# First group's ScalarE opening and small loads, the last group's bias, and one weight tile of layer one in a two-layer graph kernel

## The chip, the cores and the metric

One core of a Trainium2 chip runs the whole kernel in one launch. The metric is device time in microseconds (us). The kernel before takes 3325.39 us, the median of three runs (3324.43 to 3325.61).

## The reference

Two graph layers over 4096 nodes of 512 features, each followed by a residual and a layer norm. All data are float32; `adj` is 4096 x 4096 of zeros and ones.

```python
# layer 0: four heads of 128
support = (x @ weight).reshape(N, 4, 128)                # "s" products in the kernel
f1, f2 = support . weight_u, support . weight_v          # two numbers for each node and head
w = leaky_relu(f1 + f2, slope 0.2) * adj                 # softmax over w where it is not zero
out = softmax(w) @ support + bias + x @ proj_w + proj_b  # "b" products: x @ proj_w
x = layernorm(x + out)
# layer 1: eight heads of 64, keys, queries and values from Wks, Wqs, Wvs
scores = q k^T / 8 + 0.01 * eye - 1e16 * (1 - max(adj, eye))
x = layernorm(x + (softmax(scores) @ v) @ Wo)
```

The residual `x +` of layer 0 is put into `proj_w` as an added identity. `bias` and `proj_b` are both one row of 512 numbers, the same for each node.

## The kernel before

Everything is in `tile_gat_then_masked_attention`; the order of instructions on each engine is that of the Python code, since the schedule is manual. Semaphores between engines follow from the tiles.

**Projections.** Eight groups of 512 nodes (`for g in range(NG)`). Each group makes two results, kind `"s"` (x @ weight, kept as `s4`) and kind `"b"` (x @ (proj_w + identity), kept as `base`). Each is computed by Strassen's scheme in seven smaller products numbered 1 to 7, so a group has 14 calls of `product`, called s1, s5, ... and b1, b5, ... below. A product is eight matmul groups on TensorE (L846). Products 2, 3 and 4 accumulate on the PSUM tiles of 1, 5 and 7, after these have been read: tile 1 by a ScalarE copy (L863), tile 5 also (L863), tile 7 by VectorE (L869), after which GpSimd adds product 5 to the corner (L871). The list that gives the order is `begin` for group 0 (all s, then all b, each 1, 2, 5, 6, 7, 3, 4), `usual` for groups 1 to 6 and `end` for group 7. Products are made of sums of blocks of x (`combine_x`: sums 0 and 1 on VectorE, L797 and L799; 2 and 3 on GpSimd, L801 and L804), and sums of blocks of the weights (`combine_w`, L763), made once. `add_identity` (L895) puts the identity into `pw_sb` by sixteen small GpSimd operations.

`dots` (L817) takes the products of `s4` with `weight_u` and `weight_v` on VectorE. These two rows are loaded into `uv`, copied into PSUM by ScalarE (L928, `uv_ps`) after the seventh product of group 0, and read from there. In group 0 the four calls of `dots` come behind the eighth to eleventh product; the third of them reads the corner that GpSimd made in L871.

`bb` holds bias + proj_b: `bias` is loaded into all partitions (L677), `proj_b` is added to it by an accumulating DMA that GpSimd issues (L905). It is added to `base` by GpSimd (L879), in the last group by VectorE; then SyncE stores `base` to `base_d[g]` in DRAM (L881).

**The first loads.** ScalarE's own queue issues, in this order: four loads of the first half of `weight`, one of x, four of the second half of `weight`, two for `uv`, one for `bb`. ScalarE's first computing instruction is the copy of s1, behind them all.

**Layer 0's attention.** 16 passes (four blocks of 1024 target nodes, four heads), each of 32 steps j over the source nodes. `front(w, h, j)` makes the tile `p` of a step on VectorE (L640), and for even j the mask `az` (L635) out of signs that ScalarE makes (L624); p has four buffers. `front` runs three steps ahead of the matmuls of L1087 (`LA = 3`). For the first pass the fronts of steps 0, 1 and 2 are already called in the last group (`early`); that of step 3 is called in the loop's first turn, behind the last group's work. `beside_unit` puts other work beside the steps: adjacency blocks of the next pass are narrowed (DMA by GpSimd, L586), transposed (DMA by SyncE, L594) and copied to 8 bits by ScalarE (L600), the values of the next head are loaded (L1002). At a block's end `add_base` adds `base_d` to the result by an accumulating DMA (L1063); group 7's is read in the last block only.

**Layer 1** follows: keys, queries and values (L1248 to L1298), then 32 pairs of query group and head pair, in which TensorE makes scores (L1138) and weighted sums (L1599).

Of the kernel before, what the change touches and what calls it, by code (L numbers as in the profile page):

```python
# [8 lines left out]
F32 = mybir.dt.float32  # L9
# [3 lines left out]
AF = mybir.ActivationFunctionType  # L13
ALU = mybir.AluOpType
# [4 lines left out]
P = 128  # L19
# [410 lines left out]
def tile_gat_then_masked_attention(  # L430
# [56 lines left out]
    total = const.tile([P, NG * NP1], F32, name="total")  # L487

    base_d = [dram.tile([P, GT, D], F32, name=f"base_d{g}") for g in range(NG)]
    x1_d = [dram.tile([G, D], F32, name=f"x1_d{g}") for g in range(NG)]  # L490
    sup_d = [dram.tile([P, NT, W0], F32, name=f"sup_d{h}") for h in range(H0)]
    fr_d = [dram.tile([2, H0, W], F32, name=f"fr_d{w}") for w in range(NW)]
# [74 lines left out]
    with tc.tile_pool(name="l0", bufs=NG) as l0, \  # L567
# [77 lines left out]
        with tc.tile_pool(name="l0s", bufs=2) as sp:  # L645
# [14 lines left out]
            def load_w0(queue, dst, src, c):  # L660

                for a in range(NQ):
                    f = a * P + 2 * c * SQ
                    queue.dma_start(
                        dst[a * SQ:(a + 1) * SQ, 2 * c:2 * c + 2, :],
                        src[f:f + 2 * SQ, :].rearrange("(k r) d -> r k d", r=SQ))

            bb = sp.tile([P, D], F32, name="bb", bufs=1)
            load_w0(nc.scalar, w_sb, weight, 0)
            load_x(0, 0, HG // SQ, (nc.sync, nc.sync, nc.sync, nc.scalar))  # L670
            load_w0(nc.scalar, w_sb, weight, 1)
            load_x(0, HG // SQ, G // SQ)
            for c in range(2):
                load_w0(nc.sync, pw_sb, proj_w, c)
            for k, src in enumerate((weight_u, weight_v)):
                nc.scalar.dma_start(uv[:, k, :], on_all_partitions(src, D))
            nc.scalar.dma_start(bb, on_all_partitions(bias, D))  # L677
            load_x(1)

            def factors(g, s4):  # L680
# [41 lines left out]
            for c in range(NCJ):  # L722
# [4 lines left out]
                if c < NCJ - 3:  # L727
                    for k in range(CJ):
# [1 line left out]
                            lambda c=c, k=k: shrink(0, c, k))  # L730
            beside.setdefault(NT // 2, []).append(lambda: load_fr(0, 0))
            early = {5: lambda: signs(0, 0, 0), 8: lambda: front(0, 0, 0), 9: lambda: front(0, 0, 1),
                     7: lambda: signs(0, 0, 2), 11: lambda: front(0, 0, 2)}

            def turn_x(g, c, n=0, halves=1):

# [98 lines left out]
            def product(g, s4, kind, i):  # L835

                if i in (1, 5, 6, 7):
                    tiles[kind, i] = op.tile([P, G], F32, name="o_ps")  # L840
                out = tiles[kind, {2: 1, 3: 5, 4: 7}.get(i, i)]
                more = i in (2, 3, 4)
                xb, wb = x_of(g, i), w_of(kind, i)
                for t in range(2):
                    for c in range(2):
                        nc.tensor.matmul(out[:, t * HD:(t + 1) * HD], xb[:, c, t * P:(t + 1) * P],  # L846
                                         wb[:, c, :], start=not more and t == 0 and c == 0,
                                         stop=c == 1, skip_group_check=True)
                if i == 1:
                    if kind == "b":  # L850
                        for n in range(2):
                            base[n] = sp.tile([P, 2, D], F32, name="base", bufs=3)
                    elif g == NG - 1:
                        places = room("y_sb").rearrange("p s c r -> p s (c r)")
                        sb.update({("s", 1): places[:, 0], ("s", 5): places[:, 1],
                                   ("b", 1): places[:, 2], ("b", 5): places[:, 3]})
                    else:
                        sb.update({("s", 1): room("z"), ("s", 5): room("z"),
                                   ("b", 1): room("az"), ("b", 5): room("az")})
                u2, p5 = sb[kind, 1], sb[kind, 5]  # L860
                last = block_of(kind, s4, 1, 1)
                if i in (1, 5):
                    nc.scalar.activation(sb[kind, i], out, AF.Copy)  # L863
                elif i == 2:
                    nc.scalar.activation(block_of(kind, s4, 0, 0), as_block(out, kind), AF.Copy)
                elif i == 6:
                    nc.vector.tensor_tensor(u2, out, u2, op=ALU.add)
                elif i == 7:
                    nc.vector.tensor_tensor(last, as_block(out, kind), as_block(u2, kind),  # L869
                                            op=ALU.add)  # L870
                    nc.gpsimd.tensor_tensor(last, last, as_block(p5, kind), op=ALU.add)  # L871
                else:
                    n, m = (0, 1) if i == 3 else (1, 0)
                    nc.vector.tensor_tensor(block_of(kind, s4, n, m), as_block(out, kind),
                                            as_block(u2, kind), op=ALU.add)
                if kind == "b" and i in (3, 4):
                    n = (3, 4).index(i)
                    engine = nc.vector if g == NG - 1 else nc.gpsimd
                    engine.tensor_tensor(base[n], base[n],  # L879
                                            bb[:, None, :].to_broadcast([P, 2, D]), op=ALU.add)  # L880
                    later.at(1, lambda t=base[n]: nc.sync.dma_start(  # L881
                        base_d[g][:, 2 * n:2 * n + 2, :], t))

# [12 lines left out]

            combine_x(0, 0)
            combine_w(nc.vector, "s", (5,))
            for i in (1, 2, 3):
                combine_x(0, i)  # L900
            combine_w(nc.vector, "s", (6, 7, 4))
            for m in range(2):
                add_identity(m)
# [1 line left out]
            nc.gpsimd.dma_start(bb, on_all_partitions(proj_b, D), accum_op=ALU.add)  # L905
            uv_ps = [xp.tile([P, H0, D0], F32, name="x_ps") for _ in range(2)]
            usual = [(kind, i) for i in (1, 5, 2, 6, 7, 3, 4) for kind in ("s", "b")]
            begin = [(kind, i) for kind in ("s", "b") for i in (1, 2, 5, 6, 7, 3, 4)]
            end = [(kind, i) for kind in ("s", "b") for i in (1, 5, 2, 6, 7, 3, 4)]
            for g in range(NG):  # L910
                fs[g] = l0.tile([P, 2, GT, H0], F32, name="f")
                s4 = sp.tile([P, H0, GT, W0], F32, name="s4")
                plan = end if g == NG - 1 else usual if g else begin
                todo = {}
                for k, (i, wait, n, m) in enumerate(
                        ((2, 1, 0, 0), (3, 0, 0, 1), (7, 3, 1, 1), (4, 0, 1, 0))):
                    todo.setdefault(plan.index(("s", i)) + wait if g else 7 + k, []).append((n, m))
                for k, (kind, i) in enumerate(plan):
                    if k in (0, 3, 7, 10):
                        t = (0, 3, 7, 10).index(k)  # L920
                        if t == 1 and g + 2 < NG:
                            load_x(g + 2)
                        for fn in beside.get(g * GT + t, []):
                            fn()
                    product(g, s4, kind, i)
                    if g == 0 and k == 6:
                        for n in range(2):
                            nc.scalar.activation(uv_ps[n], uv[:, n, :].rearrange(  # L928
                                "p (h d) -> p h d", h=H0), AF.Copy)
                    for nm in todo.get(k, ()):  # L930
                        dots(g, s4, *nm)
                    if g == NG - 1 and k in early:
                        early[k]()
                    if g == NG - 1 and k == 10:
                        factors(g, s4)
                    first = 0 if g else 10
                    if g + 1 < NG and first <= k < first + KC:
                        turn_x(g + 1, k - first)
                    if g + 1 < NG and (6 <= k < 10 if g else k == 13):
                        for n in (k - 6,) if g else range(4):  # L940
                            combine_x(g + 1, n)
                    if k in (2, 6, 9, 12):
                        later.step()
                xTs.pop(g)
                x_s.pop(g)
                if g + 1 == NG:
                    later.step()
                if g + 1 < NG:
                    later.at(1, lambda g=g, s4=s4: factors(g, s4))
# [34 lines left out]
        with wait_by_tile("l0v", 2) as vp:  # L984
            pools[1] = vp, vp

            def beside_unit(w, h, j):

                n = w * H0 + h
                if n == 0:  # L990
                    for c, first in zip(range(NCJ - 3, NCJ), (9, 15, 22)):
                        if c > NCJ - 3 and j == first - 7:
                            turn_in0(0, c)
                        if first <= j < first + CJ:
                            shrink(0, c, j - first)
                    if j == LA:
                        narrow(0, NCJ - 1)
# [78 lines left out]
            for n, (w, h, j) in enumerate(steps):  # L1076
                if n + LA < len(steps):
                    beside_unit(*steps[n + LA])
                    front(*steps[n + LA])
                if j == 0:  # L1080
                    o_t[w, h] = [op.tile([P, G], F32, name="o_ps")[:, 0:BK * W0].rearrange(
                        "p (b d) -> p b d", b=BK) for _ in range((WT + BK - 1) // BK)]
# [709 lines left out]
```

## Time and profile before

| what | value |
|---|---|
| median of three runs | 3325.39 us |
| time of the profiled execution | 3324.41 us |
| its span | 3322.5 us |
| TensorE busy | 3301.6 us, 99% of the span |
| VectorE, ScalarE, GpSimd busy | 75%, 59%, 65% |
| mean granted TensorE clock | 0.998 |
| DMA, mean over the span | 184 GB/s |

The page divides the span into 40 slices. TensorE has a 9 (90% or more) in all of them but the last. The time of the profiled execution is 1.91 us more than its span. A share of busy time is a mean over stages, so the questions of this case are read from the list of TensorE's waits and from the order of time in the first 50 us, around 210 us (where layer 0's attention begins) and around 290 us (its second pass).

### The profile page before, as it was taken

To read this page: it belongs to the slowest core of one execution; us is meant where nothing else is said; L and a number is where in the kernel's file an instruction comes from. 1 tells how busy PE (TensorE), PEld (TensorE's weight loads), DVE (VectorE), ACT (ScalarE), POOL (GpSimd) and SP (SyncE) were. 2 spreads that over 40 slices of the span, in tenths; PEclk is the share of its full clock that TensorE was granted. 3 is DMA by queue.
4 is the path that set the end of the run, shared out by engine and by line. 5 is a ranking of instruction groups with operands and counts; after the bars stand their busy time and mean duration, and the time that the engine had idled before them with its cause. 6 is when DMAs were issued, how large, how long until landed. Compare 5 with 4: busy or idle time off the path is not lost.

```text
span 3322.5 us, 67217 instructions
## 1 busy us (share of the span) xinstructions
PE 3301.6 (99%) x27160; PEld 1967.0 (59%) x27160; DVE 2477.7 (75%) x3186; ACT 1947.7 (59%) x2439; POOL 2173.3 (65%) x1602
## 2 busy tenths in 40 slices
PE   9999999999999999999999999999999999999998
PEld 8899999999999777733333333333333333333333
DVE  6689899899999677467767666677666766667766
ACT  1267968878766310156656566566665656656564
POOL 5630040040030244389999999999999999999996
PEclk9999999999999999999999999999999999999999
DMA  8989796686532444489898988889889799897984
GB/s 178 227 204 183 220 182 170 153 191 147 138 93 58 104 146 125 153 221 208 193 211 224 228 195 198 209 188 259 198 197 211 187 215 242 196 210 185 214 195 112
DMA packets 398993, 612.06 MB, mean 184 GB/s; under 512 B 167632, under 2 KB 248528, under 8 KB 398672
## 3 DMA queue, kind: packets, MB, share of 16 engines
q0 software_dynamic: 97520, 258.77, 42.8%
q1 hardware_dynamic: 299280, 345.88, 33.5%
q8 instruction: 216, 3.54, 0.4%
q10 hardware_dynamic: 1872, 3.02, 0.4%
q14 instruction: 105, 0.86, 0.1%
HBM read 315.87 MB, written 109.25 MB: 128 GB/s over the span
## 4 chain that ended last, share of the span: by engine, by line
PE 97%; DVE 1%; DMA 1%; POOL 1%; issue 0%; ACT 0%; ACTq 0%; POOLq 0%; DVEq 0%
PE o_ps L1087 27%; PE o_ps L1599 26%; PE s_ps L1138 26%; PE o_ps L846 5%; PE s_ps L1663 3%; PE s_ps L1298 2%; PE s_ps L1248 2%; PE s_ps L1255 2%; PE x_ps L1255 1%; PE x_ps L1248 1%; PE s_ps L1618 1%; DMA p<-p 0%; PE s_ps L1294 0%; DMA w_sb<-in_L_gnn_weight_dram 0%; DVE p L1731 0%
## 5 line engine op out<-in xcount | busy, mean ns | idle before, releaser
L1574 POOL TENSOR_TENSOR q_sum<-q_sum,p 128x1024 f32<-128x1024 f32 x538 | 1375.6, 2557 | 64.3 <-DMA p<-p 39.5
L1554 DVE TENSOR_TENSOR p<-s_ps,adjT 128x1024 f32<-128x1024 f32 x896 | 1044.5, 1216 | 465.0 <-ACT s_ps L1551 436.2
L1551 ACT ACTIVATE s_ps<-s_ps 128x1024 f32<-128x1024 f32 x1021 | 967.2, 1006 | 594.4 <-PE s_ps L1138 591.9
L1599 PE MATMUL o_ps<-p,v_sb 64*64 64x512 f32 x8192 | 943.6, 590 | 0.0
L1138 PE MATMUL s_ps<-q_sb,k_sb 64*64 64x512 f32 x8192 | 942.9, 589 | 0.1
L1087 PE MATMUL o_ps<-sup_t,p 128*128 128x129 f32 x8192 | 915.7, 275 | 1.2 <-DVE p L640 1.2
L1087 PEld LDWEIGHTS o_ps<-sup_t,p 128*128 128x128 f32 x8192 | 915.3, 192 | 1.7 <-DVE p L640 1.4
L640 DVE SCALAR_TENSOR_TENSOR p<-fr_t,dj,az 128x1024 f32<-128x1024 f32 x512 | 650.3, 1284 | 66.9 <-PE o_ps L1087 38.8
L1599 PEld LDWEIGHTS o_ps<-p,v_sb 64*64 64x64 f32 x8192 | 310.3, 133 | 570.6 <-issue 560.6
L1138 PEld LDWEIGHTS s_ps<-q_sb,k_sb 64*64 64x64 f32 x8192 | 312.6, 133 | 566.4 <-issue 453.9
L624 ACT ACTIVATE z<-fr_t,f 128x1024 fp8e4<-128x1024 f32 x512 | 557.1, 1143 | 100.9 <-DVE az L635 100.8
L1584 POOL DMA_DIRECT2D p<-p x412 | 438.6, 1303 | 10.1 <-PE o_ps L1599 9.2
L1063 POOL DMA_DIRECT2D agg<-base_d x32 | 29.1, 1217 | 386.8 <-DMA sup_t<-sup_d 204.7
L585 POOL COPY seen<-token 128x1 f32<-128x1 f32 x24 | 10.9, 455 | 356.8 <-DVE token L583 356.8
L1554 DVE TENSOR_TENSOR p<-s_ps,md 128x1024 f32<-128x1024 f32 x128 | 150.7, 1217 | 67.8 <-ACT s_ps L1551 62.0
L635 DVE TENSOR_TENSOR az<-adjT,z 128x512 int32<-128x512 int32 x256 | 175.2, 685 | 2.1 <-ACT z L624 0.9
L600 ACT ACTIVATE adjT<-stage 128x1024 fp8e4<-128x1024 bf16 x128 | 130.9, 1051 | 18.3 <-DMA stage<-adj_d 18.2
L1663 PE MATMUL s_ps<-wo_sb,on 128*128 128x512 f32 x240 | 110.8, 604 | 0.0
L1633 ACT ACTIVATE r<-r_h 32x256 f32<-32x256 f32 x248 | 102.2, 412 | 2.9
L1049 ACT ACTIVATE agg<-o_ps,rinv 128x128 f32<-128x128 f32 x128 | 42.1, 370 | 70.5 <-DVE den L1042 46.3
L1322 ACT ACTIVATE v<-s_ps 128x256 f32<-128x256 f32 x28 | 10.7, 383 | 115.0 <-PE s_ps L1298 99.9
L1663 PEld LDWEIGHTS s_ps<-wo_sb,on 128*128 128x128 f32 x240 | 43.3, 189 | 55.9 <-issue 55.7
(275 smaller groups left out, 2236.0 us busy)
## 6 DMA issues: line engine op xcount, KB each, us to landing
p<-p POOLq DMA_DIRECT2D x412, 512.0 KB, 9.1
k_sb<-k_d SPq DMA_DIRECT2D x128, 512.0 KB
v_sb<-v_d SPq DMA_DIRECT2D x128, 512.0 KB
adj_d<-in_adj_dram POOLq DMA_DIRECT2D x32, 1024.0 KB, 11.0
sup_t<-sup_d SPq DMA_DIRECT2D x120, 258.0 KB
fr_t<-fr_d SPq DMA_DIRECT2D x16, 1024.0 KB
adjT_d<-adjT SPq DMA_DIRECT2D x32, 512.0 KB
adjT<-adjT_d SPq DMA_DIRECT2D x32, 512.0 KB
```

The lines of the kernel that those rows point to most:

```text
L624: nc.scalar.activation(z[:, k, :], fr_t[w, h][:, 0, :], AF.Sign, bias=fs[j // GT][:, 0, (j + k) % GT, h:h + 1], saturate=False)
L635: nc.vector.tensor_tensor(az.bitcast(I32), adjT[w, j // CJ][:, j % CJ:j % CJ + 2, :].bitcast(I32), z.bitcast(I32), op=ALU.bitwise_and)
L640: nc.vector.scalar_tensor_tensor(p, fr[:, 1, :], dj[j // GT][:, j % GT, h:h + 1], az_t[w, h, j // 2][:, j % 2, :], op0=ALU.max, op1=ALU.mult)
L846: nc.tensor.matmul(out[:, t * HD:(t + 1) * HD], xb[:, c, t * P:(t + 1) * P], wb[:, c, :], start=not more and t == 0 and c == 0, stop=c == ...
L1087: nc.tensor.matmul(o[t // BK][:, t % BK, :], p[:, t * P:(t + 1) * P], s, start=(j == 0 and t % BK == 0), stop=(j == NT - 1), skip_group_ch ...
L1138: nc.tensor.matmul(s[c:c + MS, e, :], k[r, a + c:a + c + MS], qt[g, m][r, :], start=True, stop=True)
L1551: nc.scalar.activation(s, s, AF.Exp, scale=float(KD) ** -0.5)
L1554: nc.vector.tensor_tensor(p, s, keep[:, None, :].to_broadcast([P, HP, G]), op=ALU.mult)
L1574: nc.gpsimd.tensor_tensor(q, q, p, op=ALU.add)
L1584: later.at(2, lambda: nc.gpsimd.dma_start(a, b, accum_op=ALU.add))
L1599: nc.tensor.matmul(o[c, n, :], v[r, j % CH, c], p[r, e, :], start=(j == 0), stop=(j == NT - 1))
L1663: nc.tensor.matmul(s, on_t[g][:, m, t * P:(t + 1) * P], wo_sb[:, m, :], start=(m == 0), stop=(m == NP1 - 1))
```

## The change

- ScalarE gets a copy of one column, before the loads of the second half of `weight` and behind those of the first.
- The loads of `weight_u`, `weight_v` and `bias` go from ScalarE's queue to GpSimd: the first two between GpSimd's parts of `combine_x` (2 and 3), the third behind part 3.
- Group 0's b products run in the order 1, 5, 2, 6, 7, 3, 4.
- In group 7 `bb` is no longer added to `base`. `bb` is stored to `bb_d` in DRAM in group 1 (SyncE), and in the second pass GpSimd issues a DMA that adds `bb_d`, repeated for the four node tiles, to `base_d[7]` in DRAM.
- The front of step 3 is called in the last group, behind product b3, and no longer in the loop's first turn. (This is the "layer one's fourth weights" of the change's name: the weights of the first attention layer.)

```diff
+    bb_d = dram.tile([P, D], F32, name="bb_d")
...
             load_w0(nc.scalar, w_sb, weight, 0)
             load_x(0, 0, HG // SQ, (nc.sync, nc.sync, nc.sync, nc.scalar))
+            nc.scalar.activation(small.tile([P, 1], F32, name="bn_ve"), ones[:, 0:1], AF.Copy)
             load_w0(nc.scalar, w_sb, weight, 1)
             load_x(0, HG // SQ, G // SQ)
             for c in range(2):
                 load_w0(nc.sync, pw_sb, proj_w, c)
-            for k, src in enumerate((weight_u, weight_v)):
-                nc.scalar.dma_start(uv[:, k, :], on_all_partitions(src, D))
-            nc.scalar.dma_start(bb, on_all_partitions(bias, D))
             load_x(1)
...
             early = {5: lambda: signs(0, 0, 0), 8: lambda: front(0, 0, 0), 9: lambda: front(0, 0, 1),
-                     7: lambda: signs(0, 0, 2), 11: lambda: front(0, 0, 2)}
+                     7: lambda: signs(0, 0, 2), 11: lambda: front(0, 0, 2), 12: lambda: front(0, 0, 3)}
...
                 if kind == "b" and i in (3, 4):
                     n = (3, 4).index(i)
-                    engine = nc.vector if g == NG - 1 else nc.gpsimd
-                    engine.tensor_tensor(base[n], base[n],
-                                            bb[:, None, :].to_broadcast([P, 2, D]), op=ALU.add)
+                    if g < NG - 1:
+                        nc.gpsimd.tensor_tensor(base[n], base[n],
+                                                bb[:, None, :].to_broadcast([P, 2, D]),
+                                                op=ALU.add)
...
             combine_w(nc.vector, "s", (5,))
-            for i in (1, 2, 3):
+            for i in (1, 2):
                 combine_x(0, i)
+            for k, src in enumerate((weight_u, weight_v)):
+                nc.gpsimd.dma_start(uv[:, k, :], on_all_partitions(src, D))
+            combine_x(0, 3)
+            nc.gpsimd.dma_start(bb, on_all_partitions(bias, D))
             combine_w(nc.vector, "s", (6, 7, 4))
...
-            begin = [(kind, i) for kind in ("s", "b") for i in (1, 2, 5, 6, 7, 3, 4)]
             end = [(kind, i) for kind in ("s", "b") for i in (1, 5, 2, 6, 7, 3, 4)]
+            begin = [("s", i) for i in (1, 2, 5, 6, 7, 3, 4)] + end[7:]
...
+                    if (g, k) == (1, 7):
+                        nc.sync.dma_start(bb_d, bb)
                     product(g, s4, kind, i)
...
                 n = w * H0 + h
+                if n == 1 and j == 4 * LA:
+                    nc.gpsimd.dma_start(base_d[NG - 1], bb_d[:, None, :].to_broadcast([P, GT, D]),
+                                        accum_op=ALU.add)
...
                     beside_unit(*steps[n + LA])
-                    front(*steps[n + LA])
+                    if n:
+                        front(*steps[n + LA])
```

## The prediction

> **What bounds the kernel now.** I read the page first, then the list of TensorE's waits, then the timeline of the three places that the change touches. The page says that TensorE is the bound throughout: busy 99% of the span.
>
> ```profile
> span 3322.5 us, 67217 instructions
> ...
> PE 3301.6 (99%) x27160; PEld 1967.0 (59%) x27160; DVE 2477.7 (75%) x3186; ACT 1947.7 (59%) x2439; POOL 2173.3 (65%) x1602
> ```
>
> So a change that leaves the matmuls alone can only win what TensorE waits, or a slow clock. All of its waits (engine, line, what it waited for, us in total, times, longest):
>
> ```profile
> PE o_ps L846 <- ACT z L863: 3.4, 1, 3.4
> PE o_ps L886 <- POOL ident masks.py:199: 1.4, 1, 1.4
> PE o_ps L1087 <- DVE p L640: 1.2, 1, 1.2
> PE s_ps L1753 <- DVE all_ok L537: 1.0, 1, 1.0
> PE o_ps L846 <- issue: 0.7, 1, 0.7
> PE s_ps L1605 <- DVE p L1731: 0.5, 1, 0.5
> PE o_ps L846 <- DVE base L869: 0.4, 1, 0.4
> ```
>
> The change touches four of the seven: 3.4, 0.7 and 0.4 in group 0, and 1.2 where attention begins; 5.7 us in all. TensorE never waits between 39.2 and 215.7 us, nor from 216.9 us to the end of layer 1, so a lead won early is carried to the end unless something new stops it.
>
> The first two places in order of time (start, us):
>
> ```profile
> 8.78 1.99 PE L846 MATMUL o_ps<-w_sb,xT 128*128 128x256 f32 x8
> 11.82 0.33 ACTq L677 DMA_DIRECT2D bb<-in_L_gnn_bias_dram  x1
> 12.19 1.28 ACT L863 ACT_TABLE_LOAD   x1 [12.19 <-DMA w_sb<-in_L_gnn_weight_dram]
> 13.48 0.60 ACT L863 ACTIVATE z<-o_ps 128x512 f32<-128x512 f32 x1
> 14.13 3.78 PE L846 MATMUL o_ps<-w_sb,xT 128*128 128x256 f32 x8 [3.36 <-ACT z L863]
> ...
> 28.76 1.39 POOL L871 TENSOR_TENSOR s<-s,z 128x512 f32<-128x512 f32 x1
> ...
> 39.16 1.97 PE L846 MATMUL o_ps<-more_w,xT 128*128 128x256 f32 x8 [0.35 <-DVE base L869]
> ```
>
> s1 is done at 10.77, but its copy starts only at 13.48: ScalarE issues small loads until 12.15 and then loads its table. And the place where attention begins:
>
> ```profile
> 211.91 1.35 DVE L879 TENSOR_TENSOR base<-base,bb 128x1024 f32<-128x1024 f32 x1
> ...
> 214.42 1.23 DVE L879 TENSOR_TENSOR base<-base,bb 128x1024 f32<-128x1024 f32 x1 [0.56 <-POOL base L871]
> ...
> 215.56 1.28 DVE L640 SCALAR_TENSOR_TENSOR p<-fr_t,dj,az 128x1024 f32<-128x1024 f32 x1
> ...
> 216.90 33.30 PE L1087 MATMUL o_ps<-sup_t,p 128*128 128x129 f32 x294 [1.20 <-DVE p L640]
> ```
>
> Step 3's p stands behind both bias additions, one of which waits for GpSimd.
>
> **Two rules of the Trainium skill.** "ScalarE: Activation LUTs", section "What ACT_TABLE_LOAD costs", gives a load of about 1283 ns plus about 1380 ns of draining. The trace shows 1.28 us and the copy at once behind it (13.48), no drain; I go by 1.28. "TensorE: Matmul & The Clock Gate", Part 1, says that the clock halves after an idle window of about 3.4 us and comes back after a busy one, the windows running freely. In the windows view the clock falls inside 12.80 to 13.00 and is back inside 19.60 to 19.80, 6.8 us apart, which fits two windows; but it fell 2.1 us into the idle time, so a part-idle window was enough. I cannot read the threshold, so I cost group 0 with and without the slow clock.
>
> **Group 0, TensorE's side.** A product takes 1.72 us at full clock (group 1's start at 40.96, 42.69 and 44.41). The table load now runs behind ScalarE's x load (ends 4.25), until about 5.7 with the small copy (0.2, by the 128x16 copies of 0.20 to 0.22); the second half of the weights starts then and not at 5.44. The chain of waits has its third load issued at 7.59, landed 4.22 later; the fourth was issued at about 8.3, so landed about 12.5 (an estimate; 14.13 at most, since s2 ran then). I keep 12.5: the later loads' issues are spaced out to 8.3, far past 5.7. So z is copied by 11.4, s2 waits for weights and starts at 12.5, 1.6 earlier. If the clock stays up: s2 ends 14.2; s5 waits for VectorE's weight sum (14.19 + 0.68) until 14.9; s6 to s4 follow to 23.5, against 27.3. If the clock halves until 19.65 as before, s2 takes until 16.0, s5 until 19.4, and s4 ends at about 26.4. Then the b order: before, b2 came straight behind b1's copy and stood 0.9 us; now b5 stands between. b4 can start six products behind s4's end: 33.8 at full clock (34.0 with b5's weight sum), 36.7 with the slow clock; 37.6 even if all of s gained nothing. Before: 39.16.
>
> **Group 0, GpSimd's side.** This side takes work and decides. b4 accumulates on b7's tile and so waits for VectorE's L869. In VectorE's order that stands behind the third and fourth dots, and the third waits for GpSimd's L871, which ended at 30.15. GpSimd's list gains three DMA issues. The nearest row is L905: 1.07 us, with the next instruction 0.81 behind it; the p<-p issues of layer 1, at 1303 ns, bound it above. The two for `uv` stand at 13.73, where GpSimd idled 1.83 us waiting for VectorE's L799: L804 moves from 15.55 to about 15.9, 0.3 late. The `bb` issue adds 1.0. Sixteen identity adds (5.69) and four weight sums (5.1) follow, then L905, then L871: its end moves to 31.5 (30.9 at 0.8 an issue, 32.2 at 1.3). From there VectorE needs eight dots (1.66), b6's addition (0.65), eight dots (1.66), a transpose (0.65), L869 (0.65): 36.8. So b4 starts at 36.8, **2.4 us earlier** (1.7 to 2.9), nearly whatever the clock does. Behind it s1 of group 1 (38.6) needs a transpose done at 37.4, and s5 (42.0) a sum done at about 40.9: neither is late.
>
> **What group 0 newly waits for.** ScalarE's copy of `uv` (two of 0.59) stands ahead of b1's copy. Issued by GpSimd at 13.7 and 14.7, into DMAs that are 1.05 to 1.2 busy until 28, `uv` lands at perhaps 21 to 26: L905's 256 KB took 4.6 us, adj_d's 1 MB 10.6. b2 needs b1's copy by 27.2, and dots has room until L871's end; nothing is lost up to about 27. `bb` must have landed before L905 (29.3), 11 us after its issue; behind L905 on GpSimd stand L871, the narrowing of adjacency and the base additions. The three issues that ScalarE loses cost it nothing: it waits for TensorE from then on.
>
> **Where attention begins.** VectorE loses 1.35 + 1.23 and the 0.56 wait. p of step 3 comes right behind L874 of b3 (211.88): 211.9 to 213.2, ahead of the 215.7 at which TensorE wants it, so **the 1.2 us goes**. Next is step 4: L874 of b4 to 213.9, az 0.69, p 1.28: 215.9, wanted at 215.7 + 1.84 = 217.5. After that VectorE needs 1.6 a step against TensorE's 1.84. The whole scene moves with TensorE, since VectorE's work there starts from the s products.
>
> **Edits at nothing.** The `bb_d` store is one SyncE issue of about 0.35 (the base_d store's 345 to 360 ns) at about 52 us, `bb` long landed. The DRAM accumulation: GpSimd's queue is idle beside the narrowings in the second pass (issues at 279.99, 288.97), its operands were stored long before, and what stands behind it on GpSimd, two narrowings, is used 50 steps later. Its traffic is the question. The software queue's 258.77 MB took 42.8% of the engines' time, 5.5 us per MB, so up to 6 us of backlog at 281 to 297, ahead of the transpose issued at 295.58, for which ScalarE waited until 304.84. The signs behind that copy had 1.8 us to spare (ended 307.97, used at 309.75) and p about 3.9 (three steps less its own making): 5.7 in all. I take 0; 0.5 us if the backlog is whole.
>
> **Sum.** 2.4 + 1.2 = 3.6 us, against the profiled execution's 3324.41 (span 3322.5 plus 1.91): 3320.8. The median shown is 0.98 above that execution. I put the median at 3321.3, half of it kept. Bounds of the two terms: 2.9 to 4.1 won.
>
> **Rivals.**
> 1. *As summed* (0.60): 3321.3; its own range is 3320 to 3322.8.
> 2. *One of the two gains doesn't come* (0.17): the second half of the weights slips with the table load, or GpSimd's issues take longer, and only attention's 1.2 us remains: 3323.7; or group 0 wins and step 3's p is late: 3322.5. For it: DMAs saturated until 28 us. Against: b's order alone still gives 1.5.
> 3. *The loads through GpSimd land late* (0.11), which ends slower. `uv` landing at T lets b4 start at T + 1.2 + 32 dots (6.6) + 3 x 0.65, about T + 9.8. It costs nothing below 27, takes all that is won at 30.6, and by 36 makes the kernel 5 us slower. Equally `bb`: L905 would hold GpSimd until it lands. Against: the landing times above. I price it at 3326 to 3328.
> 4. *The accumulation stops the second pass* (0.06): a transpose over 9.3 us later than now takes back everything; the backlog of 6 says no. 3325 to 3327.
> 5. *More is won* (0.06): GpSimd's issues hide, the clock stays up: TensorE's own side would give 5.2 + 1.2, 3318.
>
> Leaving out the ends of 3 and 5, the range is 3318.8 to 3326.0. A difference of 0.2%, 6.6 us, is about what can be told from none here: a gain over that exceeds all that TensorE's waits hold in these places bar the slow clock, a loss needs rival 3 at its worst. Faster 0.06, same 0.87, slower 0.07.
>
> **What will show it.** Right: ACT_TABLE_LOAD at about 4.3; the wait of 3.4 for z shrunk to under 2, on a DMA of w_sb; b4 of group 0 at about 36.8, still waiting for L869; L871's first at 31.5; no wait of L1087 on p near 213; TensorE without waits at 285 to 330. Wrong: ScalarE waiting for `uv` past 27, GpSimd idle before L905, L871 later than 33.9 (where group 0 wins nothing), a TensorE wait on p in the second pass, or new waits of group 1 on x, whose loads I took as unmoved.

## The result: 0.36% slower, and one new wait

Before: median 3324.91 us in the paired runs. After: 3337.04 us. The ratio is 1.0036, 95% interval 1.0026 to 1.0047, which is 12.1 us by the medians. The forecast was 3321.3 us, in a range that ended at 3326.0: wrong in size and sign. The profiled execution took 3334.6 us.

From the page of the kernel after, and its list of TensorE's waits (engine, line, what it waited for; us in total, times, longest). In it L1097 is the attention matmul (L1087 before), L845 the matmul of the projections (L846) and L641 makes `p` (L640):

```profile
span 3332.8 us, 67215 instructions
...
PE o_ps L1097 <- DVE p L641: 12.9, 1, 12.9
PE o_ps L845 <- DVE p L796: 2.6, 1, 2.6
PE o_ps L886 <- POOL ident masks.py:199: 1.4, 1, 1.4
...
PE o_ps L845 <- DVE base L868: 0.4, 1, 0.4
```

A wait of 12.9 us is new; the other new ones are of 0.5 us or less. Of the four waits that the change was to touch, the 0.7 of b2 and the 1.2 where attention begins are gone, the 3.4 became 2.6, and the 0.4 stayed.

The new wait lies in the second pass. The chain of what ended last, followed back inside 280 to 335 us (start, us, what):

```profile
279.97 9.86 PE o_ps L1097 x89
289.83 27.54 DMA stage<-adj_d
...
317.45 1.06 ACT adjT L601
318.51 2.08 ACT z L625 x2
...
320.62 0.70 DVE az L636
...
321.41 1.30 DVE p L641
...
322.75 12.32 PE o_ps L1097 x90
```

The transposed load of one adjacency block, 1 MB issued by SyncE, took 27.54 us. Behind it hang ScalarE's copy to 8 bits, the signs, the mask, `p`, and at 322.75 TensorE. In the kernel before the same load was issued at 295.58, and ScalarE copied at 304.84 after a short wait (timeline of before; in brackets the idle time ahead and its releaser):

```profile
304.84 1.06 ACT L600 ACTIVATE adjT<-stage 128x1024 fp8e4<-128x1024 bf16 x1 [2.91 <-DMA stage<-adj_d]
```

The same stretch in the timeline of after, with the added DMA:

```profile
275.04 1.27 POOL L997 DMA_DIRECT2D base_d<-bb_d  x1
283.34 0.78 POOL L587 DMA_DIRECT2D adj_d<-in_adj_dram  x1
...
292.12 0.75 POOL L587 DMA_DIRECT2D adj_d<-in_adj_dram  x1
...
317.45 1.06 ACT L601 ACTIVATE adjT<-stage 128x1024 fp8e4<-128x1024 bf16 x1 [21.27 <-DMA stage<-adj_d]
```

The adding DMA is issued 15 us ahead of the transposed load, and between them and behind stand two of the usual narrowings. What the wait costs beyond itself is in the windows of after (window, length, busy time of PE, PEld, DVE, ACT, POOL, then TensorE's granted clock, DMA share, GB/s):

```profile
312.00:314.00 2.00, 0.00 (x0) 0.00 (x0) 0.00 (x0) 0.00 (x0) 0.00 (x0) 0.83 1.26 68
314.00:326.00 12.00, 3.25 (x15) 3.25 (x16) 4.48 (x5) 8.55 (x9) 0.00 (x0) 0.50 0.69 101
326.00:328.00 2.00, 2.00 (x16) 2.00 (x16) 2.00 (x3) 2.00 (x3) 0.00 (x0) 0.76 0.64 262
```

TensorE stood idle, its clock was halved inside the wait, and after the wait it worked 3.25 us at 0.50 and 2.00 at 0.76: 1.6 + 0.5 = 2.1 us more. "TensorE: Matmul & The Clock Gate" of the Trainium skill, Part 1, has this rule (idleness halves the clock, work brings it back); here it came back about 4 us after work resumed.

The gains came, and in this execution more than forecast. Timeline of after, group 0:

```profile
4.13 1.28 ACT L672 ACT_TABLE_LOAD   x1 [4.13 <-DMA w_sb<-in_L_gnn_weight_dram]
11.04 0.60 ACT L862 ACTIVATE z<-o_ps 128x512 f32<-128x512 f32 x1 [5.41 <-DMA w_sb<-in_L_gnn_weight_dram]
13.64 1.96 PE L845 MATMUL o_ps<-w_sb,xT 128*128 128x256 f32 x8 [2.64 <-DVE p L796]
28.04 1.40 POOL L870 TENSOR_TENSOR s<-s,z 128x512 f32<-128x512 f32 x1
34.95 1.97 PE L845 MATMUL o_ps<-more_w,xT 128*128 128x256 f32 x8 [0.35 <-DVE base L868]
```

The table load is at 4.13, no longer behind the loads; s1 is copied at 11.04 instead of 13.48; b4 starts at 34.95 instead of 39.16, 4.2 us earlier. In both kernels it still waits for the tile of b7. And the start of attention (timeline of after, VectorE and TensorE):

```profile
207.58 1.46 DVE L641 SCALAR_TENSOR_TENSOR p<-fr_t,dj,az 128x1024 f32<-128x1024 f32 x1
...
205.97 14.23 PE L1097 MATMUL o_ps<-sup_t,p 128*128 128x129 f32 x126
```

Attention starts at 205.97 against 210.17, and the 1.2 us wait inside it does not occur: a lead of 5.4 us. So the spans should differ by 12.9 + 2.1 - 5.4 = 9.6 us; they differ by 10.3. 0.7 us is not accounted for. The profiled execution is the fastest of the six, and its lead in group 0 is not the usual one: eight other profiles with the same group 0 show 2.3 to 2.7 us in place of the 4.2 (below).

### The profile page after: what moved, and what is told of

It is laid out like the page before. It is cut to its first block, busy times and chain, and to the rows that moved or that the text cites. A ratio compares the mean times of both kernels' runs of the same rounds, so it can differ in the third digit from the quotient of the medians.

```text
span 3332.8 us, 67215 instructions
## 1 busy us (share of the span) xinstructions
PE 3300.6 (99%) x27160; PEld 1966.4 (59%) x27160; DVE 2475.0 (74%) x3184; ACT 1948.2 (58%) x2440; POOL 2177.6 (65%) x1606
## 4 chain that ended last, share of the span: by engine, by line
PE 97%; DMA 2%; DVE 1%; POOL 1%; issue 0%; ACT 0%; ACTq 0%; POOLq 0%; DVEq 0%
PE o_ps L1097 27%; PE o_ps L1609 26%; PE s_ps L1148 26%; PE o_ps L845 5%; PE s_ps L1673 3%; PE s_ps L1308 2%; PE s_ps L1258 2%; PE s_ps L1265 2%; PE x_ps L1265 1%; DMA stage<-adj_d 1%; PE x_ps L1258 1%; PE s_ps L1628 1%; DMA p<-p 0%; PE s_ps L1304 0%; DVE p L1741 0%
## 5 line engine op out<-in xcount | busy, mean ns | idle before, releaser
L1097 PE MATMUL o_ps<-sup_t,p 128*128 128x129 f32 x8192 | 917.4, 275 | 12.9 <-DVE p L641 12.9
L1097 PEld LDWEIGHTS o_ps<-sup_t,p 128*128 128x128 f32 x8192 | 917.1, 192 | 13.2 <-DVE p L641 13.0
L641 DVE SCALAR_TENSOR_TENSOR p<-fr_t,dj,az 128x1024 f32<-128x1024 f32 x512 | 649.2, 1284 | 62.4 <-PE o_ps L1097 33.6
```

The source lines that it names most:

```text
L641: nc.vector.scalar_tensor_tensor(p, fr[:, 1, :], dj[j // GT][:, j % GT, h:h + 1], az_t[w, h, j // 2][:, j % 2, :], op0=ALU.max, op1=ALU.mult)
L1097: nc.tensor.matmul(o[t // BK][:, t % BK, :], p[:, t * P:(t + 1) * P], s, start=(j == 0 and t % BK == 0), stop=(j == NT - 1), skip_group_ch ...
```

## The experiments

Two theories for the stall. **The added DMA as traffic**: 1 MB more on GpSimd's queue delays what comes after it. **Something particular to it**: that it accumulates, or that it reads one row many times. A third possibility is that another part of the same change is to blame. For each run the figures given are ScalarE's wait for the transposed load (2.91 us before, 21.27 after) and TensorE's wait for `p` in the second pass (none before, 12.9 after). In the kernels that copy or halve the addition, all or half of the last group goes without its bias.

### Which part of the change it is

All of the change without the bias part (VectorE adds the bias in the last group, nothing is added in DRAM):

```diff
-                    if g < NG - 1:
-                        nc.gpsimd.tensor_tensor(base[n], base[n], ...)
+                    engine = nc.vector if g == NG - 1 else nc.gpsimd
+                    engine.tensor_tensor(base[n], base[n], ...)
...
-                if n == 1 and j == 4 * LA:
-                    nc.gpsimd.dma_start(base_d[NG - 1], ..., accum_op=ALU.add)
```

> The changed kernel with the bias part undone: the last group's bias is added on VectorE again, no bb_d, no adding DMA in the second pass. Theory 'the adding DMA': the 12.9 us wait of L1097 and the slow clock behind it go, group 0 keeps its 4.2 us and attention's start its 1.2, so about 5.4 us faster than before: 3319.5. Rival 'the earlier start': group 0 runs 4 us earlier and meets the narrowing DMAs at a worse moment, so the second pass stalls without the adding DMA too: 3330 to 3337.

Measured: 3323.82 us, ratio 0.9996 (0.9988 to 1.0005). No stall: ScalarE waited 2.66 us. But the gain was smaller than expected, since one of TensorE's waits stayed (list of waits of this kernel; L1090 is the attention matmul):

```profile
PE o_ps L1090 <- DVE p L640: 1.9, 1, 1.9
```

With the bias additions back on VectorE, TensorE waits for p again (at 217 us), although the front of step 3 is called in the last group. And b4 started at 36.81: group 0 gained 2.3, not 4.2. The clock is the difference. The same 2 us in the windows of after and of this kernel (columns as above):

```profile
14.00:16.00 2.00, 2.00 (x11) 1.77 (x10) 2.00 (x4) 0.36 (x1) 1.46 (x2) 1.00 1.05 221
...
14.00:16.00 2.00, 2.00 (x6) 1.54 (x6) 2.00 (x4) 0.00 (x0) 1.45 (x2) 0.50 1.06 221
```

After is the exception. In all eight other profiles with this group 0 the clock was at 0.5 for a part of 12 to 20 us, and b4 starts at 36.43 to 36.84.

The kernel before with the bias part alone:

```diff
-                    engine = nc.vector if g == NG - 1 else nc.gpsimd
-                    engine.tensor_tensor(base[n], base[n], ...)
+                    if g < NG - 1:
+                        nc.gpsimd.tensor_tensor(base[n], base[n], ...)
...
+                    if (g, k) == (1, 7):
+                        nc.sync.dma_start(bb_d, bb)
...
+                if n == 1 and j == 4 * LA:
+                    nc.gpsimd.dma_start(base_d[NG - 1], ..., accum_op=ALU.add)
```

> The kernel before with the bias part alone (bb_d, no addition in the last group, the adding DMA in the second pass); group 0 and the front of step 3 as before. Theory 'the adding DMA': it stalls alone, a wait of TensorE on p of 10 to 18 us near 310 to 325 us and some 3 us of half clock, less up to 1.2 us at attention's start: 3337 to 3342. Rival 'the earlier start': no stall here, 3324 to 3325.

Measured: 3334.05 us, 1.0026 (1.0016 to 1.0037), less than the expected 3337. In the profiled execution, one of the longest (3341.92 us), the stall is there in full, with ScalarE waiting 21.35 us (waits of this kernel):

```profile
PE o_ps L1094 <- DVE p L641: 12.9, 1, 12.9
```

There is no wait at 216 us: taking the two additions off VectorE is enough for attention's 1.2 us. The single times go from 3324.33 to 3342.46, wider than those of the other kernels (at most 11.4 us apart), which suggests that the stall is not the same in each execution.

The kernel after, with the addition in the fourteenth pass instead of the second:

```diff
-                if n == 1 and j == 4 * LA:
+                if n == 13 and j == 4 * LA:
```

> The changed kernel with the same adding DMA issued in the fourteenth pass instead of the second, where DMAs are 0.13 to 0.16 busy and nothing is transposed or narrowed. Theory 'the adding DMA beside the transposes': no stall, all gains kept, 3319.5. Rival 'the earlier start': still a stall in the second pass, 3330 to 3337. Rival 'the addition costs wherever it is': slower than the kernel without the bias part by several us.

Measured: 3321.35 us, 0.9986 (0.9979 to 0.9993), with TensorE not waiting at all in the second pass and ScalarE 3.87 us (timeline of this kernel):

```profile
301.80 1.06 ACT L601 ACTIVATE adjT<-stage 128x1024 fp8e4<-128x1024 bf16 x1 [3.87 <-DMA stage<-adj_d]
```

It falls short of the expected 3319.5, which counted on 4.2 us in group 0; here b4 starts at 36.84, 2.3 us earlier than before. One number moved brings the change to the good side. Accumulating and reading one row often are harmless there, so the place decides.

### What it is about the place

A plain copy of the repeated row into a scratch tensor, at the change's place:

```diff
+    copy_d = dram.tile([P, GT, D], F32, name="copy_d")
...
-                    nc.gpsimd.dma_start(base_d[NG - 1], bb_d[:, None, :]..., accum_op=ALU.add)
+                    nc.gpsimd.dma_start(copy_d, bb_d[:, None, :].to_broadcast([P, GT, D]))
```

> The changed kernel with a plain copy of the same bytes (bb_d repeated four times, 1 MB, DRAM to DRAM, into a scratch tensor) on the same queue at the same place instead of the addition; the last group's bias is left out of the output. Theory 'the gap': the transposing load at 290 us is fast only while GpSimd's queue has no copies in flight, so any megabyte there that pushes the two narrowings behind it closes part of the gap: the copy takes 6 to 10 us instead of 17, the narrowings end 7 to 10 us sooner, the stall shrinks but a rest of 0 to 6 us may stay: 3320 to 3327. Rival 'the addition itself' (reading back its destination disturbs the transpose): no stall at all, 3319.5. Rival 'bytes ahead of it': as the addition, 3337.

The same with another source (each row read once):

```diff
+                    nc.gpsimd.dma_start(copy_d, base_d[0])
```

> The changed kernel with a plain copy of 1 MB from base_d[0], each byte read once, into a scratch tensor in the place of the addition (the last group's bias is left out of the output). Theory 'a lag of the queue': much as the copy of the repeated row, whose ScalarE wait was 13.7 us and TensorE wait 5.3: 3323 to 3329. Rival 'the repeated row': no slow transpose, ScalarE waits under 5 us, 3320 to 3322.

And half of the addition, 0.5 MB:

```diff
-                    nc.gpsimd.dma_start(base_d[NG - 1], bb_d[:, None, :].to_broadcast([P, GT, D]),
+                    nc.gpsimd.dma_start(base_d[NG - 1][:, 0:2, :], bb_d[:, None, :].to_broadcast([P, 2, D]),
```

> The changed kernel with half of the adding DMA (two of the four node tiles, 0.5 MB; the other half of the last group's bias is left out of the output). Theory 'GpSimd's queue gets no gap in which its slowest DMA engine catches up, and the transpose goes at that engine's pace': half the bytes leave half the lag; ScalarE waits 8 to 13 us for the first transposed block instead of 21.3, TensorE 0 to 5 instead of 12.9: 3320 to 3328. Rival 'any addition there sets off the slow mode': as the whole one, 3333 to 3337.

| put at the change's place | ScalarE's wait | TensorE's wait | median | ratio to before |
|---|---|---|---|---|
| nothing (addition in pass 14) | 3.87 | none | 3321.35 | 0.9986 (0.9979 to 0.9993) |
| addition, 0.5 MB | 8.79 | 0.4 | 3322.65 | 0.9988 (0.9982 to 0.9995) |
| copy, 1 MB, other source | 11.79 | 3.4 | 3327.90 | 1.0004 (0.9996 to 1.0013) |
| copy, 1 MB, repeated row | 13.68 | 5.3 | 3328.53 | 1.0010 (1.0003 to 1.0017) |
| addition, 1 MB | 21.27 | 12.9 | 3337.04 | 1.0036 (1.0026 to 1.0047) |

The waits are those of one profiled execution each. For the copy of the repeated row (timeline and waits of this kernel; L1097 is the attention matmul):

```profile
311.55 1.06 ACT L602 ACTIVATE adjT<-stage 128x1024 fp8e4<-128x1024 bf16 x1 [13.68 <-DMA stage<-adj_d]
...
PE o_ps L1097 <- DVE p L642: 5.3, 1, 5.3
```

Bytes alone make a stall. The repeated row makes 1.9 us of the wait in these two profiles, and 0.6 us between the medians. The copy of the repeated row came out 1.5 us above its expected range; the other two fell inside theirs. Half of the addition fits into the slack. That it accumulates adds 7.6 us of wait to the copy's 13.68, and 8.5 us to its median; all three profiles with a whole addition in this pass show 20.57 to 21.35. The adding DMA took longer to land: 17.1 us from issue, the copy 14.8. While its packets moved, the core's DMAs carried 207 GB/s (285 to 291 us of after), against 397 for the copy (287 to 289 us), so it holds the queue longer. Why it costs that much more was not settled.

Then the reverse: the kernel before, no byte added, but two of its own narrowings issued in successive steps instead of five apart:

```diff
-                        if u == (13 + 5 * (c - 3) if w else 16 + 5 * c) and ...
+                        if u == (13 + 5 * (c - 3) if w else 16 + 5 * c if c < 6 else 42 + c) and ...
```

> The kernel before, no adding DMA and no byte more, but the same two narrowing DMAs issued at steps 48 and 49 instead of 46 and 51, so that both are in flight when the transposing load of step 50 begins and its gap between them is gone. Theory 'copies beside the transpose slow each of its packets': ScalarE waits for the transposed block by 8 to 18 us more than the 2.9 of before and TensorE waits 4 to 12 us near 310 us: 3328 to 3338. Rival 'the adding DMA': no stall, 3324 to 3326.

Measured: 3329.08 us, 1.0011 (1.0004 to 1.0017); its timeline and waits:

```profile
312.48 1.06 ACT L600 ACTIVATE adjT<-stage 128x1024 fp8e4<-128x1024 bf16 x1 [10.07 <-DMA stage<-adj_d]
...
PE o_ps L1087 <- DVE p L640: 2.9, 2, 1.7
```

ScalarE's wait went from 2.91 to 10.07, and of the two waits of TensorE the 1.7 is new. Both are smaller than expected, and 1.7 us is less than half of the 3.6 that the ratio stands for; the rest is open. But the stall needs no added DMA. And the kernel after, with the addition left where it is and the last two narrowings of the block issued later, at steps 60 and 68:

```diff
-                        if u == (13 + 5 * (c - 3) if w else 16 + 5 * c) and ...
+                        if u == (13 + 5 * (c - 3) if w else 16 + 5 * c if c < 6 else 8 * c + 12) and ...
```

> The changed kernel, the adding DMA where it is, but the second block's last two narrowing DMAs issued 14 and 17 steps later (steps 60 and 68 of the block's count instead of 46 and 51; they are transposed at 98 and 106). Theory 'the narrowings pushed into the transpose': the first transposing load (step 50) then has only the adding DMA's last 3 us beside it, lands within some 12 us, no wait of TensorE: 3319 to 3321. Rival 'the adding DMA itself slows the transpose': the stall of 12.9 us stays in large part, 3330 to 3337.

Measured: 3321.78 us, 0.9988 (0.9981 to 0.9994), 0.8 above the expected range. TensorE did not wait in this pass, and ScalarE hardly (timeline of this kernel):

```profile
299.34 1.06 ACT L601 ACTIVATE adjT<-stage 128x1024 fp8e4<-128x1024 bf16 x1 [1.36 <-DMA stage<-adj_d]
```

The same addition at the same place costs nothing when no narrowing is pending behind it.

Last, the addition ten steps earlier, to give it more time:

```diff
-                if n == 1 and j == 4 * LA:
+                if n == 1 and j == 2:
```

> The changed kernel with the adding DMA at step 2 of the second pass instead of step 12, so that four narrowing DMAs with the gaps between them (8.8 us from one issue to the next, some 6 us of work) lie between it and the transposing load. Theory 'a lag that gaps make good': ScalarE waits 2 to 6 us for the first transposed block, TensorE not at all: 3320 to 3323. Rival 'any addition in this pass': a stall of several us stays, 3327 to 3337.

Measured: 3336.23 us, 1.0030 (1.0020 to 1.0041), and the stall stands (timeline and waits of this kernel):

```profile
318.21 1.06 ACT L601 ACTIVATE adjT<-stage 128x1024 fp8e4<-128x1024 bf16 x1 [20.57 <-DMA stage<-adj_d]
...
PE o_ps L1097 <- DVE p L641: 12.2, 1, 12.2
```

The expectation missed: I took it that GpSimd's queue had gaps in which it would catch up. In 280 to 294 us of this kernel the queue's packets hold 121.7% of the engines' time (shares count overlapping packets), and its earlier windows show no gap from 264 us on: until about 280 us SyncE's load of the next head's values, 2 MB, shares the engines with it. A backlog made early is carried along.

### What happens to the transposed load

The queues' lines (packets, MB, share of the time of 16 engines): q1 is SyncE's queue with the transposed load, q0 GpSimd's. After, 298 to 303 us:

```profile
q1 hardware_dynamic: 658, 0.17, 84.6%
q0 software_dynamic: 340, 0.35, 53.1%
```

The copy for the addition, 300 to 304 us:

```profile
q1 hardware_dynamic: 612, 0.16, 127.5%
q0 software_dynamic: 38, 0.04, 5.7%
```

Before, 298 to 301 us, where q0 has no line:

```profile
q1 hardware_dynamic: 2740, 0.70, 126.4%
```

The last two narrowings later, 293 to 297 us:

```profile
q1 hardware_dynamic: 4052, 1.03, 121.0%
q0 software_dynamic: 4, 0.01, 0.9%
```

The mean time of a packet is share x 16 x window / packets. A packet of the transposed load has about 256 bytes (0.70 MB / 2740):

| kernel, window | transposed packet | transposed load, MB in us | GpSimd's queue |
|---|---|---|---|
| before, 298 to 301 | 22 ns | 0.70 in 3 | empty |
| last two later, 293 to 297 | 19 ns | 1.03 in 4 | 0.9% |
| after, 298 to 303 | 103 ns | 0.17 in 5 | 53.1% |
| copy for the addition, 300 to 304 | 133 ns | 0.16 in 4 | 5.7% |

With GpSimd's queue empty the block comes in about 4 us. With a copy of GpSimd's pending, its packets take five to seven times as long, even where that queue moves nearly nothing: 5.7% is about what a single engine of the 16 would show. Nor is it bandwidth: in 312 to 314 us of after, all queues together moved 68 GB/s. In before, GpSimd's queue drained at about 297 us, and the load ran alone before the next narrowing's copy came; an added megabyte closes that moment. The load and the narrowing then drag on together: the narrowing issued at 292.12 landed 23.0 us later, the load at 317.4.

The packet counts suggest how this comes about. Where GpSimd's narrowing runs beside SyncE's load of values, the two queues move equally many packets, as if they took turns (addition ten steps earlier, 268 to 274 us):

```profile
q0 software_dynamic: 584, 0.60, 58.5%
q1 hardware_dynamic: 586, 1.08, 55.2%
```

In the copy's window above, GpSimd's 38 packets took about one engine's time, and 612 transposed packets are 38 for each of 16 engines. In the window of after, 340 packets over 53.1% of 16 engines are 40 for each of these 8.5 engines, and 658 / 16 is 41. The copy of the other source shows the same in 300 to 305 us: 47 packets at 5.6%, and 770 / 16 = 48. So the counts fit a transposed load that advances on all its engines together, at the pace of those that still take turns with GpSimd's packets: 8 to 10 packets a us on each engine, against 71 alone (1133 / 16 in 298 to 299 us of the copy of the other source). At 8 to 10 a us the block's 256 packets on each engine would take 26 to 32 us, an estimate from these counts; the load took 27.5 from its issue.

"DMA: Bandwidth & Descriptors" of the Trainium skill, section "Issuing engines are not separate DMA queues", says that all these transfers run on the same 16 engines and interleave. The trace agrees, and the equal counts show how evenly. The same page, "Latency and other measured facts", says that two of the engines are usually slower, with GpSimd's descriptors as a suspected cause. One straggling engine would fit the copy's 5.7%. The profile does not name the engine of a packet, and in single microseconds of after the transposed packets vary from 2 to 20 for each engine, so the mechanism is inferred from counts, not shown.

### Group 0 and the start of attention, part by part

Four of these five kernels ran once each and are read for their traces. ScalarE's first operation alone, on the kernel before:

```diff
+            nc.scalar.activation(small.tile([P, 1], F32, name="bn_ve"), ones[:, 0:1], AF.Copy)
```

> The kernel before with ScalarE's first operation alone. The table load is out of the way but the small loads still stand on ScalarE's queue until about 12.8: z copied at 12.8 instead of 14.1, s2 0.6 to 1.3 earlier than the 14.1 to 15.0 of before. Rival 'the loads alone matter': s2 as before.

The moved loads alone, on the kernel before:

```diff
-            for k, src in enumerate((weight_u, weight_v)):
-                nc.scalar.dma_start(uv[:, k, :], on_all_partitions(src, D))
-            nc.scalar.dma_start(bb, on_all_partitions(bias, D))
...
+            for k, src in enumerate((weight_u, weight_v)):
+                nc.gpsimd.dma_start(uv[:, k, :], on_all_partitions(src, D))
...
+            nc.gpsimd.dma_start(bb, on_all_partitions(bias, D))
```

> The kernel before with only the three small loads moved to GpSimd. If the loads are what held ScalarE: z is copied at about 11.1 instead of 13.5, s2 starts at 13.5 to 13.9 instead of 14.1 to 15.0, and b4 of group 0 at 37.5 to 38.3 instead of 39.0 to 39.2 (b2 still waits 0.7 for b1's copy). If ScalarE's operation is what counts: s2 as before.

The order of the b products alone, on the kernel before:

```diff
+            begin = [("s", i) for i in (1, 2, 5, 6, 7, 3, 4)] + end[7:]
```

> The kernel before with group 0's b order alone. b2's wait of 0.7 goes; b4 waits for VectorE's L869, which waits for b7: b4 0.5 to 0.9 earlier than the 39.0 to 39.7 of before. Rival 'GpSimd's side decides': b4 where it was, the wait only moved to it.

The version with the addition in pass 14, without ScalarE's operation:

```diff
-            nc.scalar.activation(small.tile([P, 1], F32, name="bn_ve"), ones[:, 0:1], AF.Copy)
```

> The kernel with the adding DMA in the fourteenth pass, without ScalarE's first operation. The small loads being gone from ScalarE's queue, its table load can run at about 8.7 to 10 us, before s1 is done (11.1), and the second half of the weights is issued 0.2 us sooner. Theory 'the operation does nothing': z copied at 11.1, s2 at 13.5 to 13.8, same time within 0.03%, 3321.3. Rival 'the operation hides the table load': z 1 to 2 us later, s2 by up to 0.5, 3322 to 3323.

The same version, with step 3's front back in the loop:

```diff
-                     7: lambda: signs(0, 0, 2), 11: lambda: front(0, 0, 2), 12: lambda: front(0, 0, 3)}
+                     7: lambda: signs(0, 0, 2), 11: lambda: front(0, 0, 2)}
...
-                    if n:
-                        front(*steps[n + LA])
+                    front(*steps[n + LA])
```

> The kernel with the adding DMA in the fourteenth pass, with the front of step 3 back in the loop's first turn. Theory 'the bias additions alone held step 3': no wait of L1097's line at about 212 us, 3320 to 3323. Rival 'the moved front is what removes it': a wait of 0.5 to 1.2 us there.

| kernel | s1's copy | s2 starts | b4 starts | time |
|---|---|---|---|---|
| before | 13.48 | 14.13 | 39.16 | 3324.41 |
| operation alone | 12.37 | 13.60 | 37.38 | 3324.07 |
| loads alone | 11.35 | 13.34 | 37.31 | 3323.29 |
| order alone | 13.84 | 14.48 | 38.88 | 3326.94 |
| after | 11.04 | 13.64 | 34.95 | 3334.60 |
| after, addition in pass 14 | 11.19 | 13.85 | 36.84 | 3321.54 |

The times are those of the profiled executions. The operation and the loads are two ways to the same gain: either puts s2 at 13.3 to 13.6. With both, s2 is no earlier (13.64), so s1's copy no longer sets it. In the last row, which has b's order too, b4 is another 0.5 us earlier; the 34.95 of after is the execution whose clock stayed up. Without the operation (addition in pass 14) the table load stands at 9.20 and s2 at 13.37, and the time is 3321.13 us, 0.9988 (0.9981 to 0.9995), against 0.9986 with it: beside the moved loads the operation wins nothing measurable. The order alone removes b2's 0.7 us, but b4, which waits for VectorE's tile, starts only 0.3 earlier, less than expected, in an execution whose s2 was itself 0.35 late. With step 3's front in the loop (3323.68 us, one execution) there was no wait for p at attention's start: the moved front does nothing; the bias additions alone had held step 3.

The versions of 3321.13 and 3321.35 us beat both kernels, by 0.12 to 0.14% against before.

## Why the prediction was wrong

**The failed step** is the adding DMA among the edits at nothing: "I take 0; 0.5 us if the backlog is whole". It was 12.9 us of wait and 2.1 us of slow clock. The backlog of up to 6 us was priced as bytes that stand ahead of the transposed load, so it stayed near the slack of 5.7. That backlog is the term that was mis-sized: ScalarE's wait grew by 18.4 us (21.27 against 2.91). The load was not shifted by 6 us; it became three times as long, 27.5 us against 9.3. By the counts above it seems to go at the pace of the engines that still take turns with GpSimd's packets, for as long as there is one, and not by the bytes ahead of it.

The other term, the slack of 5.7, was right. What ScalarE waited above 2.91, less 5.7, is 12.7 us for the whole addition, 5.1 and 3.2 for the two copies, 1.5 for the two narrowings together and 0.2 for half of the addition; TensorE waited 12.9, 5.3, 3.4, 1.7 and 0.4.

The queues' lines of before held a hint that I did not read: in 298 to 301 us only q1 moves, at 22 ns a packet, and it is that empty moment which the addition uses up.

**Rival 4** named this place and the sign, and from which delay on it takes back everything ("over 9.3 us later"), but not the slower packets. Its chance of 0.06 and its price, 3325 to 3327, came from the same backlog of 6.

**Group 0: the forecast of 36.8 for b4 came true in most profiles, but by another path, and that is luck.** The eight other profiles with group 0 as in after have b4 at 36.43 to 36.84, 2.3 to 2.7 us earlier than before. In them the clock fell, and TensorE worked without a wait from s2 to the end of b7: it is TensorE's side, put at 36.7 for a slow clock (with s2 over 1 us too early and a longer slow stretch), that decides, and not GpSimd's, put at 36.8. In after the clock stayed up, and b4 came at 34.95, so "nearly whatever the clock does" was wrong by about 1.9 us. GpSimd's side was mis-sized: an issue of a small load took 0.56 to 0.78 us, not 0.8 to 1.3, and the corner addition that closes its list ended at 29.44, not 31.5; from there to b4 it took 5.5 us, near the 5.3 of the forecast. TensorE's start was worse than forecast: s2 at 13.64 and not 12.5. The `uv` rows had landed by 21.4, at the early end of 21 to 26, so rival 3 did not come.

**The start of attention: right, 1.2 us, for one of its two reasons.** Taking the additions off VectorE gave it all; calling step 3's front earlier gave nothing.

**The sum** of 3.6 us holds when the addition is put where the queue can take it: 3321.35 against 3325.92, 4.6 us by the medians (2.3 to 7.0 by the interval of the ratio). The profile of that kernel shows 2.3 in group 0 and the 1.2 where attention begins, 3.5 us.

## What to carry to other kernels

Before a DMA is added "where its queue is idle", look at how the queue stands at the next transfer that has a deadline: whether it is empty then, and whether that transfer slows down when it is not. A delay of a transfer is not priced by the bytes ahead of it alone; compare its packet times in the windows with and without company. And move one number, the place of the new work, before giving up the change: here it turned 0.36% slower into 0.14% faster.

## Hardware behaviour that I had not expected

- A transposed load beside a pending copy of GpSimd's: 103 to 133 ns a packet of 256 bytes, against 19 to 22 ns alone, and 27.5 us for 1 MB; once with GpSimd's queue at only 5.7% of the engines' time.
- A transposed load seems to advance in step on all its engines: with GpSimd's queue at about one engine's time, 612 transposed packets on 16 engines went by with 38 of GpSimd's, 38 an engine.
- An accumulating DMA of 1 MB from DRAM to DRAM cost the wait for the transposed load beside it 7.6 us more than a copy of the same size (21.27 against 13.68).
- The clock after an idle stretch of 2.6 us in group 0 stayed up in after, and fell to 0.5 in all eight other profiles with the same group 0 (2.5 to 2.9 us idle). What decides it stays open.
